# Row buffers by a falling look-ahead, one load for two quads' bases, and a moved base row in a gather-and-scatter graph layer

## The chip, the cores and the metric

The kernel runs on one core of a Trainium2 chip. The metric is the time of one execution on the device in microseconds (us). Three runs of the kernel before gave 1079.93, 1080.61 and 1087.88 us; the median, 1080.61 us, is the time before. Names in the text: PE is the matrix engine (PEld its weight loads), DVE the vector engine, ACT the scalar engine, POOL the GpSimd engine, which here issues the indirect DMAs, and SP the engine that issues most other DMAs.

## The reference

The layer has N = 12500 nodes with 128 features and 400000 edges, sorted by destination. Only edges of length up to 10 count.

```python
rbf = exp(-(d[:, None] - centers) ** 2 / (2 * width * width))       # 50 centres
cut = 0.5 * (cos(pi * d / 10) + 1) * (d <= 10)
W = (silu(rbf @ fw1 + fb1) @ fw2 + fb2) * cut[:, None]
messages = (h[src] @ pw + pb) * W
agg = segment_sum(messages, dst, num_segments=N)
out = layernorm(x + (h + silu(agg @ mw1 + mb1) @ mw2 + mb2))        # h is x
```

## The kernel before, in words

**Packing.** Most edges are too long and are dropped. The edges are cut into seven chunks. `pack_first` (chunk 0) and `pack(c)` shift the edges that stay to the front of each row on DVE, and `columns` writes them as lists to DRAM with one indirect DMA per chunk, the scatter at L470 on POOL's queue. `unpack(c)` (L778) reads the lists back and turns them into what the main loop needs: the source numbers `srci`, the places `dl` of the destinations counted from a base, the factors `cut`, and the row of bases `base_i`. `to_places` (L866) turns an array on PE in one of four PSUM banks and copies it out on DVE (L874); before this change the base row has a turn of its own in another bank (L909 to L913, copy at L912).

**Quads.** The main loop (from L1439) takes 139 quads of 512 edges in order. For quad q it needs the 512 source rows, which POOL gathers with four indirect DMAs of 128 rows (`fetch`, L1009, the DMA at L1015; in eight of the quads the first 128 rows come one by one through SP at L1005 instead), and the filter W from PE and ACT (lines L1056 to L1082). `message(q)` (L1086) multiplies the two on DVE (L1093). `place(q)` (L1100) writes the matrix of destinations, `sum_up(q)` (L1117) multiplies messages by it on PE (L1125), and `add(q)` (L1144) adds the sums into `aggT` at the columns that start at the base, on DVE (L1148). The base is a number in a register: `base_of` (L1130) loads it from `base_i` on DVE's queue (L1134), one load for each window, and a quad has one window up to quad 68 and two from quad 69.

**Row buffers.** `place_of(q)` says which of 21 row buffers quad q is gathered into. Thirteen are `quad_sb`, eight are the tiles `x4_sb` that hold node rows before and after. Up to quad 62 the buffers go round, `q % 21`; from quad 63 nine of them go round. `before_it(q)` is the quad that had the buffer before: the gather of q cannot start until the message of that quad has read it. `room(q)` is how far the gathers may be written into the program ahead of the messages. POOL's queue is in order: gathers in the order of the quads, with the seven scatters between them.

**The order.** The order of the instructions of each engine is fixed when the program is written, by a planner that keeps estimated times: `clock` for DVE, `pool` for POOL, `awake[c]` for the moment from which chunk c's generator may go on. `pack_until` lets the chunks' generators run in the gaps; each `yield` hands back an estimated time. At the end of `pack(c)` chunk 0 is made ready at once (`awake[0] = 0.0`, L774).

**Chunk 0's arrays.** `paired` (L813) keeps chunk 0's placement arrays in the row buffers of quads 11 and 12 (L818): `part`, `f_src` and `f_dl` in that of quad 11, `length`, `two` and `inside` in that of quad 12.

After quad 70 the node layers (lines L1156 to L1212) run between the quads, and a short tail of them follows the last quad.

Of the kernel before, what the change touches and what calls it, by code (L numbers as in the profile page):

```python
# [20 lines left out]
P = 128  # L21
# [29 lines left out]
GOT = 13  # L51
# [18 lines left out]
A_ROW = .58  # L70
AT_ONCE = 32
FROM_BANK = 3


DONE = (0.162, 4.9)
# [5 lines left out]
def kernel(  # L81
# [37 lines left out]
    nc = tc.nc  # L119
    N, H = x.shape  # L120
# [67 lines left out]
    ident = keep.tile([P, P], F32, name="ident")  # L188
    make_identity(nc, ident)
    quad_sb = [keep.tile([P, QT, H], F32, name=f"quad{k}") for k in range(GOT)]  # L190
# [87 lines left out]
    turns, end = (keep.tile([P, 1], F32, name=k) for k in ("turns", "end"))  # L278
# [54 lines left out]
    dl = keep.tile([P, NP, 2], F32, name="dl")  # L333
    base_i = keep.tile([1, NP], I32, name="base_i")
# [24 lines left out]
    def bank(own=None):  # L359

        while not free:
            go_on(next(c for c in held if c != own))
        return free.pop(0)
# [29 lines left out]
    clock = [4.3]  # L393
# [3 lines left out]
    awake = [0.0] * NC_  # L397
# [2 lines left out]
    most = [FROM_X]  # L400
    times = [0]

    def place_of(q):
        n, later = LATER
        return q % len(quad_sb) if q < n else later[(q - n) % len(later)]

    def before_it(q):

# [2 lines left out]
    def room(q):  # L411

        n = q
        while n < NL and before_it(n) < q:
            n += 1
        return n
# [17 lines left out]
    def columns(c, nodes, r_d, first, D, CAP, at_i):  # L434
# [6 lines left out]

        late_c = c >= FROM_BANK
        if late_c:
# [43 lines left out]
    def reach(c, b, bits):  # L487
        return min(ROWS[c] - (1 << b), CAPS[c] + sum(1 << j for j in range(b + 1, bits)))
# [171 lines left out]
    def pack(c):  # L660
# [4 lines left out]
        def rowed(dt, name, n=R, bufs=1):  # L665
            return work.tile([P, max(n, R_MAX) if n == R else max(CAPS)], dt, name=name,
                             bufs=bufs)[:, :n]
# [3 lines left out]
        nc.vector.tensor_copy(first, r_dst[:, 0:1])  # L671
        late_c = c >= FROM_BANK
        if late_c:
# [14 lines left out]
        step = aside.bitcast(I32)[:, :R] if late_c else rowed(I32, "step")  # L688
# [45 lines left out]
        for b in range(bits):  # L734
# [11 lines left out]
            n, k = reach(c, b, bits), 1 << b  # L746
# [24 lines left out]

        yield from columns(c, nodes, r_d, first, 0, CAP, at_i)
        awake[c] = pool[0] + (2.2 if c == 1 else 3.0)
        awake[0] = 0.0  # L774
        yield 0
        yield from unpack(c)

    def unpack(c):  # L778
# [4 lines left out]
        p0, p1 = 2 * QB[c] + (DIRECT // 2 if c == 0 else 0), 2 * QB[c + 1]  # L783
        np_ = p1 - p0
# [28 lines left out]
        def paired(dt, name):  # L813
            if c == 0:
                k = OWN_0[name]
                if k > 3:
                    return dl_0[:np_, k % 2 * 2:k % 2 * 2 + 2].rearrange("p a f -> p (a f)").bitcast(dt)
                v = quad_sb[GOT - 1 - k // 2].rearrange("p j f -> p (j f)").bitcast(dt)  # L818
                return v[:np_, k % 2 * 256:k % 2 * 256 + 256]
            return work.tile([64, 256], dt, name=name, bufs=1)[:np_]  # L820

# [17 lines left out]
        def turned():  # L839
            t = bank()  # L840
            held.append(c)
            return t, t.rearrange("p (j e) -> p j e", j=2)

        def back(t):
            held.remove(c)
            free.append(t)

        def later(more=0.0):

            if c or known[0] >= DIRECT // QT:  # L850
                awake[c] = clock[0] + (5.0 if known[0] >= QB[c + 1] else 1.0 if c == 0 else 2.5) + more
                return 0.0
            return 0.5
# [3 lines left out]
        def lengths():  # L857

            if c < 2:
                alike_in(1)  # L860
            one_of(length, 1)
            for a, b in parts(np_):
                nc.sync.dma_start(near_d[p0 + a:p0 + b], length[a:b].bitcast(F32))
            stored.add(c)

        def to_places(f, to):  # L866
            t, tp = turned()
            for j in range(2):
                nc.tensor.transpose(tp[:, j, :np_], f[:, j * P:(j + 1) * P], ident[:np_, :np_])
            if to is srci:  # L870
                lengths()
                yield 1.4 if c < 2 else 0.8
            yield later(-2.0 if c == 1 and to is srci else 0.0)
            nc.vector.tensor_copy(to[:, p0:p0 + np_, :].rearrange("p r j -> p j r"),  # L874
                                  tp[:, :, :np_])
            back(t)

        yield from to_places(f_src, srci)
# [7 lines left out]
        if mine:  # L886
            at_row = work.tile([64, P], I32, name="at_row", bufs=2)
            nc.vector.tensor_scalar(at_row[:np_], f_src[:, :P], float(4 * H), None, op0=OP.mult)
            for q in mine:
                p = 2 * (q - QB[c])  # L890
# [3 lines left out]
        base = work.tile([64, 1], F32, name="base", bufs=4)[:np_]  # L894
# [3 lines left out]
        if c < WIDE_C:  # L898
            t, tp = turned()
            nc.tensor.matmul(tp[:np_, 0, 0:1], even[:np_, :np_], base, start=True, stop=True)  # L900
            yield later()
            base = work.tile([64, 1], F32, name="base", bufs=4)[:np_]
# [3 lines left out]
        f_dl = paired(F32, "f_dl")  # L906
        nc.vector.tensor_scalar(f_dl, part, base, None, op0=OP.subtract)
        yield from to_places(f_dl, dl)
        t, tp = turned()  # L909
        nc.tensor.matmul(tp[0:1, 0, :np_], base, ident[:np_, :np_], start=True, stop=True)  # L910
        yield later()
        nc.vector.tensor_copy(base_i[:, p0:p0 + np_], tp[0:1, 0, :np_])  # L912
        back(t)  # L913
        yield 2.2
        mark = paired(F32, "mark")
        nc.vector.tensor_scalar(mark, two, float(1 << 2 * SB), -1.0, op0=OP.is_ge, op1=OP.mult)
        if c:
# [62 lines left out]
    def own(q, name, also):  # L980

        k = q % (4 if q >= OWN_4 else 2)
        if k > 1:
            return quad_sb[OTHERS[2 * also + k - 2]]
        if (name, k) not in own_sb:
            own_sb[name, k] = keep.tile([P, QT, H], F32, name=f"{name}{k}")
        return own_sb[name, k]
# [56 lines left out]
    def chunk_of(q):  # L1044
        return max(c for c in range(NC_) if QB[c] <= q)
# [63 lines left out]
    def wide(q):  # L1109

        return WIDE_0 if q < DIRECT // QT else WIDTHS[chunk_of(q)]

    def windows(q):

        return 1 if chunk_of(q) < WIDE_C else 2
# [10 lines left out]
                             start=(j % n == 0), stop=(j % n == n - 1))  # L1126

    bases = {}

    def base_of(q, ks=(0, 1)):  # L1130
        for k in ks:
            if k == windows(q):
                break
            _, v = nc.values_load_multi_w_load_instructions(  # L1134
                base_i[0:1, 2 * q + k:2 * q + k + 1], engines=[mybir.EngineType.DVE],
                min_val=0, max_val=N - wide(q),
                skip_runtime_bounds_check_because="bases are destinations, and end in the table")
            bases[q, k] = v[0]
# [197 lines left out]
    def go_on(c):  # L1336
        v = next(chunks[c], None)
        if v is None:
            todo.remove(c)
        else:  # L1340
            clock[0] += v
# [97 lines left out]
    for q in range(NL - 1):  # L1439
        while todo and q + 2 >= DIRECT // QT and todo[0] <= chunk_of(min(q + 2, NQ - 1)):  # L1440
            go_on(todo[0])
        msg = message(q)
        nodes(q)
        most[0] = room(q)
        fetches(clock[0], most[0])
        fetches(math.inf, min(NL, q + AHEAD + 1))
        assert fetched[0] > QT * min(NL - 1, q + AHEAD)
        if q >= CLEAR_Q:
            clear()
        if loads_later and q >= 8:  # L1450
            nc.sync.dma_start(*loads_later.pop(0))
        radials(q // 2 + 5)
        one_by_one()
        multiplies(q + 1 + EARLY_X)
        if q + 2 < NL:
            second(q + 2)
        if q % 4 < 2 and 2 * octs(q) < NL:
            first(octs(q))
            silu(octs(q))
        if q % 4 == 3:  # L1460
            for o in (q // 4 * 2 + 4, q // 4 * 2 + 5):
                if 2 * o < NL:
                    basis(o)
        if q > NL - 5:
            keep_busy(2)
        sum_up(q, msg)
        now = range(added(q), added(q + 1))
        for k in now:
            base_of(k, (0,))
        if q < NL - 2:  # L1470
            place(q + 1)
        if q == NL - 4:
            place(NL - 1)
        if q == NL - 2:
            for j in range(QT - 1):
                sum_up(NL - 1, message(NL - 1, (j, j + 1)), (j,))
        for k in now:
            base_of(k, (1,))
            if q == NL - 5 and k == now[0]:
                deep.append(deviations([80], st_of[0]))  # L1480
                nc.scalar.activation(warm, half_pi, AF.Silu)
            add(k)
        tail(q)
        clock[0] = max(clock[0], there_at[q])
        summed[q] = clock[0] + 0.7
        clock[0] += 2.2 + 0.3 * (windows(q) - 1)
        if q == 0:
            clear_packed(2, nc.sync)
        if todo:
            pack_until(max(there_at[q + 1], clock[0] + (PACK_US if known[0] >= QB[3] else EARLY_US)), NC_)  # L1490
        if NODES - 8 <= q < NODES - 2:
            part_of(*(("mb1", mb1_f) if q < NODES - 5 else ("mb2", mb2_f)), (q - NODES + 8) % 3)
        if not todo and not counted:
            counted.append(q)
            count()
        elif counted and some is None and fetched[0] >= QT * NL:
            some = nc.values_load(bad_i[0:1, 2:3], min_val=0, max_val=3 * E)
    q = NL - 1
# [131 lines left out]
```

## Time and profile before

| what | value |
|---|---|
| median of three runs | 1080.61 us |
| the profiled execution, its own time | 1084.51 us |
| its span, from the first to the last instruction | 1082.7 us |
| mean granted clock of PE | 0.774 |
| indirect DMAs on POOL | 548 gathers, 7 scatters |

How to read the views: a row of a timeline has the start, the length, the engine, the line, the operation, what it writes and reads, and in brackets how long the engine was idle before it and what ended that. "DVE msg L1093" in brackets means that the wait ended with the message multiplication of that line. A row of the table by stages has a stretch of time and for each engine the time it was busy in it, with the number of instructions.

### The profile page before, as it was taken

Reading aid. Unit: us, or ns where it says so; the run is one execution under the profiler, and the core shown is the slowest. Engines: PE = TensorE matmul, PEld = TensorE weight load, DVE = VectorE, ACT = ScalarE, POOL = GpSimd, SP = SyncE. Lnnn points to the kernel's source line nnn. Section 1 sums busy time; section 2 is a strip of 40 time slices with the busy share of each in tenths; the row PEclk is TensorE's granted clock in tenths of the full one; section 3 lists DMA queues with packets and bytes.
Section 4 is the critical chain, followed back from the end, with each engine's and each line's share of the span. In section 5 each row is a group of like instructions: output and inputs, shape, how many; then the busy total and the mean of one; then the engine's idle time right before and its main releaser. Section 6 shows DMA issues by size and latency. Waiting matters only on the chain. (4 is left out here: it accounts for less than half of the span.)

```text
span 1082.7 us, 13636 instructions
## 1 busy us (share of the span) xinstructions
PE 676.0 (62%) x3531; PEld 527.4 (49%) x3531; DVE 564.8 (52%) x1734; ACT 401.6 (37%) x571; POOL 530.3 (49%) x569
## 2 busy tenths in 40 slices
PE   3665437517464817455788466777766768476785
PEld 3664226406353616334666345555554556354564
DVE  8346509514454816346689465454443534253376
ACT  3334313205222324213445332353352354235365
POOL 6335732456464453754332654655555666563500
PEclk8778557858686957758889877797887878778798
DMA  7563321132222211221212223323222223223312
GB/s 221 183 220 117 112 69 38 40 83 77 57 67 57 79 50 55 71 68 48 84 55 66 76 77 78 85 63 107 78 86 89 81 77 90 72 75 99 86 59 82
DMA packets 53104, 91.38 MB, mean 84 GB/s; under 512 B 13824, under 2 KB 20576, under 8 KB 53018
## 3 DMA queue, kind: packets, MB, share of 16 engines
q1 hardware_dynamic: 34610, 53.34, 15.4%
q0 software_dynamic: 17840, 36.77, 13.2%
q8 instruction: 30, 0.49, 0.2%
q14 instruction: 56, 0.46, 0.1%
q10 hardware_dynamic: 568, 0.33, 0.1%
HBM read 74.59 MB, written 15.79 MB: 83 GB/s over the span
## 5 line engine op out<-in xcount | busy, mean ns | idle before, releaser
L1015 POOL DMA_INDIRECT quad<-proj,srci x405 | 383.7, 947 | 329.9 <-issue 109.4
L1082 PEld LDWEIGHTS bank<-fw_sb,s 128*128 128x128 f32 x1112 | 180.5, 229 | 152.5 <-issue 144.7
L1105 DVE TENSOR_SCALAR hot<-iota_n,dl,cut 128x80 f32<-128x80 f32 (+4 forms) x408 | 110.8, 333 | 203.6 <-remote 107.4
L1071 ACT ACTIVATE s<-ph 128x1024 f32<-128x1024 f32 x70 | 71.2, 1017 | 391.9 <-remote 204.2
L1065 PE MATMUL ph<-rbf,w_sb 102*128 102x512 f32 x278 | 169.5, 738 | 62.3 <-ACT s L1071 45.0
L1082 PE MATMUL bank<-fw_sb,s 128*128 128x128 f32 x1112 | 182.6, 313 | 33.9 <-issue 33.7
L1125 PEld LDWEIGHTS sums<-hot,msg 128*128 128x128 f32 x816 | 120.6, 215 | 79.7 <-issue 56.5
L1125 PE MATMUL sums<-hot,msg 128*128 128x80 f32 (+4 forms) x816 | 121.6, 294 | 37.0 <-issue 24.5
L1079 PE MATMUL bank<-fb_b,ones_b 96*128 96x512 bf16 x139 | 61.7, 444 | 103.7 <-DVE r_d L485 31.8
L1065 PEld LDWEIGHTS ph<-rbf,w_sb 102*128 102x128 f32 x278 | 59.3, 236 | 115.2 <-issue 65.0
L1015 POOL DMA_INDIRECT x<-proj,srci x95 | 90.3, 951 | 49.6 <-issue 26.5
L1148 DVE TENSOR_TENSOR aggT<-aggT,sums 128x80 f32 (+4 forms) x209 | 53.7, 257 | 111.3 <-remote 49.8
L327 PEld LDWEIGHTS bank<-pw_sb,xT 128*128 128x128 f32 (+1 forms) x292 | 50.2, 245 | 64.3 <-issue 41.9
L1093 DVE TENSOR_TENSOR msg<-bank,quad 128x512 f32<-128x512 f32 (+1 forms) x78 | 52.7, 676 | 41.7 <-issue 26.9
L1056 ACT ACTIVATE rbf<-d,rbf_bias,rbf_scale 102x512 f32<-102x512 f32 x70 | 56.2, 802 | 23.4 <-DMA d<-near_d 13.9
L1015 POOL DMA_INDIRECT quad<-in_x_dram,srci x48 | 46.3, 964 | 35.2 <-issue 13.7
L327 PE MATMUL bank<-pw_sb,xT 128*128 128x128 f32 (+1 forms) x292 | 50.9, 331 | 7.5 <-ACT xT L951 7.5
L1093 DVE TENSOR_TENSOR quad<-bank,quad 128x512 f32<-128x512 f32 (+2 forms) x40 | 25.1, 631 | 48.3 <-remote 24.5
L324 PE MATMUL bank<-pb_b,ones_b 96*128 96x512 bf16 (+2 forms) x38 | 17.6, 463 | 51.8 <-issue 22.4
L1125 PE MATMUL sums<-quad,quad 128*128 128x128 f32 (+3 forms) x296 | 46.3, 304 | 5.8 <-issue 5.4
L327 PEld LDWEIGHTS bank<-mw_sb,zs 128*128 128x128 f32 x196 | 32.3, 236 | 34.9 <-issue 18.9
L1125 PEld LDWEIGHTS sums<-quad,quad 128*128 128x128 f32 x296 | 43.9, 224 | 6.9 <-issue 5.9
(268 smaller groups left out, 881.3 us busy)
## 6 DMA issues: line engine op xcount, KB each, us to landing
d<-near_d SPq DMA_DIRECT2D x70, 256.0 KB
dl<-proj SPq DMA_DIRECT2D x1024, 0.5 KB
x<-in_x_dram SPq DMA_DIRECT2D x46, 256.0 KB
quad<-proj,srci POOLq DMA_INDIRECT x405
proj<-hp SPq DMA_DIRECT2D x24, 256.0 KB
out_dram<-x SPq DMA_DIRECT2D x22, 256.0 KB
x<-proj,srci POOLq DMA_INDIRECT x95
r_d<-in_edge_weight_dram SPq DMA_DIRECT2D x5, 256.0 KB
```

Source lines behind the costliest of these rows:

```text
L324: nc.tensor.matmul(to[:m, a:a + c, :], ones_b[:, :m], bias_b[:, :c, :], start=True, stop=False)
L327: nc.tensor.matmul(to[:m, k, :], lT[:, k * P:k * P + m], w, start=False, stop=(k == a + c - 1))
L1015: nc.gpsimd.indirect_dma_start(out=got[:, j, :], out_offset=None, in_=proj if table is None else table, in_offset=bass.IndirectOffsetOnAxi ...
L1056: nc.scalar.activation(rbf[:u], d[:u], AF.Square, bias=rbf_bias[:u], scale=rbf_scale[:u])
L1065: nc.tensor.matmul(ph[:, h, :], w1_sb[:2 * KR, h, :], rbf[:2 * KR], start=True, stop=True)
L1071: nc.scalar.activation(s[:, :n], ph[:, :n], AF.Silu)
L1079: nc.tensor.matmul(pu, ones_b[:, :P], bias_b["fb2"].rearrange("k j f -> k (j f)"), start=True, stop=False)
L1082: nc.tensor.matmul(pu[:, j * H:(j + 1) * H], s[:, j * P:(j + 1) * P], fw2_sb, start=False, stop=(j == QT - 1))
L1093: nc.vector.tensor_mul(msg[:, a:b, :], pu_of[q].rearrange("p (j f) -> p j f", j=QT)[:, a:b, :], got_of[q][:, a:b, :])
L1105: nc.vector.tensor_scalar(hot[:, j, :wide(q)], iota_n[:, :wide(q)], dl[:, at[0], at[1]], cut[:, at[0], at[1]], op0=OP.is_equal, op1=OP.mult)
L1125: nc.tensor.matmul(pa[:, k * W:k * W + wide(q)], msg[:, j, :], hot[:, j, :wide(q)], start=(j % n == 0), stop=(j % n == n - 1))
L1148: nc.vector.tensor_add(to, to, pa[:, k * W:k * W + wide(q)])
```

## The change

It does five things. (1) `place_of` chooses a buffer by a look-ahead `cap`: 20 quads up to quad 33, then one less for every four quads, down to 4 from quad 94; among the allowed buffers whose last quad lies at least `cap` back it takes the one used most recently, and if there is none the one used longest ago. (2) `paired` keeps chunk 0's `part`, `f_src` and `f_dl` in the message tile of odd quads, not in quad 11's row buffer. (3) At the end of `pack(c)` chunk 0 is made ready four planner-us later. (4) `to_places` for `dl` also turns the base row, in the same bank, and copies it right behind; the turn of its own goes. (5) `bases_of` loads the bases of two quads in one load where both have the same width and number of windows, before `place`; else `base_of` stays.

```diff
+LATE_0 = 4.0
...
+    placed = []
+
     def place_of(q):
         n, later = LATER
-        return q % len(quad_sb) if q < n else later[(q - n) % len(later)]
+        while len(placed) <= q:
+            k = len(placed)
+            last = {}
+            for m, b in enumerate(placed):
+                last[b] = m
+            allowed = range(len(quad_sb)) if k < n else later
+            cap = max(4, min(20, 20 - (k - 30) // 4))
+            ok = [b for b in allowed if last.get(b, -99) <= k - cap]
+            never = [b for b in allowed if b not in last]
+            if k < len(quad_sb):
+                placed.append(k)
+            elif ok:
+                placed.append(max(ok, key=lambda b: last.get(b, -99)))
+            else:
+                placed.append(min(allowed, key=lambda b: last.get(b, -99)))
+        return placed[q]
...
-        awake[0] = 0.0
+        awake[0] = clock[0] + LATE_0
...
-                v = quad_sb[GOT - 1 - k // 2].rearrange("p j f -> p (j f)").bitcast(dt)
+                v = quad_sb[GOT - 1] if k < 2 else own(1, "msg", 0)
+                v = v.rearrange("p j f -> p (j f)").bitcast(dt)
...
+            if to is dl:
+                nc.tensor.matmul(tp[0:1, 0, P:P + np_], base, ident[:np_, :np_], start=True, stop=True)
             yield later(-2.0 if c == 1 and to is srci else 0.0)
             nc.vector.tensor_copy(to[:, p0:p0 + np_, :].rearrange("p r j -> p j r"),
                                   tp[:, :, :np_])
+            if to is dl:
+                nc.vector.tensor_copy(base_i[:, p0:p0 + np_], tp[0:1, 0, P:P + np_])
             back(t)
...
         yield from to_places(f_dl, dl)
-        t, tp = turned()
-        nc.tensor.matmul(tp[0:1, 0, :np_], base, ident[:np_, :np_], start=True, stop=True)
-        yield later()
-        nc.vector.tensor_copy(base_i[:, p0:p0 + np_], tp[0:1, 0, :np_])
-        back(t)
-        yield 2.2
+        yield 2.4
...
+    def bases_of(quads_now):
+
+        a, n = quads_now[0], 2 * len(quads_now)
+        step = 2 // windows(a)
+        _, v = nc.values_load_multi_w_load_instructions(
+            base_i[0:1, 2 * a:2 * a + n].rearrange("o (w t) -> o w t", t=step)[:, :, 0],
+            engines=[mybir.EngineType.DVE], min_val=0, max_val=N - wide(quads_now[-1]),
+            skip_runtime_bounds_check_because="bases are destinations, and end in the table")
+        for i, (q, k) in enumerate((q, k) for q in quads_now for k in range(windows(q))):
+            bases[q, k] = v[i]
...
         now = range(added(q), added(q + 1))
-        for k in now:
-            base_of(k, (0,))
+        at_once = len(now) == 2 and wide(now[0]) == wide(now[1]) and windows(now[0]) == windows(now[1])
+        if at_once:
+            bases_of(list(now))
+        else:
+            for k in now:
+                base_of(k, (0,))
...
         for k in now:
-            base_of(k, (1,))
+            if not at_once:
+                base_of(k, (1,))
```

## The prediction

> **What bounds the kernel now.** I read the page first, then POOL's waits, then the stages in which POOL gathers without a pause.
>
> ```profile
> span 1082.7 us, 13636 instructions
> PE 676.0 (62%) x3531; PEld 527.4 (49%) x3531; DVE 564.8 (52%) x1734; ACT 401.6 (37%) x571; POOL 530.3 (49%) x569
> ```
>
> No engine is busy for more than 62% of the span, so the time lies in waits. Gathers are not late and take the same time throughout:
>
> ```profile
> DVE msg L1093 <- DMA quad<-proj,srci: 6.7, 3, 2.7
> POOL quad L1015 <- DVE msg L1093: 104.5, 21, 20.3
> ...
> L1015 POOL DMA_INDIRECT quad<-proj,srci x405: 938/944/1187, 105.0 to 1027.9; - x135
> ```
>
> Messages waited for gathers 6.7 us in all, while POOL waited for messages, that is for a free row buffer, 104.5 us. POOL is ahead and stands at the limit of its buffers. What hurts is what a run of gathers does to the others. Back to back, gathers start every 1.25 us (0.94 and a gap of 0.30). Ten runs of twelve gathers between 588 and 976 us, first the first 8 us of each (two rows and the sum), then the stretch from 9 to 16.5 us behind its start:
>
> ```profile
> core 0: us, PE busy (x) PEld busy (x) DVE busy (x) ACT busy (x) POOL busy (x), PEclk, DMA share, GB/s
> 607.90:615.90 8.00, 8.00 (x46) 7.54 (x46) 7.71 (x26) 6.41 (x9) 6.17 (x7) 0.68 0.44 114
> 959.50:967.50 8.00, 5.70 (x38) 4.47 (x37) 7.14 (x27) 0.21 (x1) 6.15 (x7) 1.00 0.27 79
> sum 80.00, PE 72.02 PEld 57.19 DVE 67.15 ACT 34.77 POOL 61.70; mean PE 7.20 PEld 5.72 DVE 6.71 ACT 3.48 POOL 6.17
> ```
>
> ```profile
> 616.90:624.40 7.50, 1.51 (x10) 1.05 (x8) 0.00 (x0) 0.00 (x0) 4.42 (x5) 0.92 0.20 54
> 968.50:976.00 7.50, 4.84 (x14) 2.74 (x15) 0.00 (x0) 2.57 (x3) 4.46 (x5) 0.58 0.19 53
> sum 75.00, PE 24.62 PEld 16.30 DVE 8.23 ACT 15.53 POOL 44.65; mean PE 2.46 PEld 1.63 DVE 0.82 ACT 1.55 POOL 4.47
> ```
>
> DVE is busy 84% of the heads (67.15 of 80) and 11% of the tails (8.23 of 75); PE falls from 90% to 33%. So a run of gathers is harmless for some 9 us and then brings the other engines nearly to a stand until it has ended. The cause is not in these rows; the rule is. Long runs cost most. Three of them, from the ninth us on, and the messages within the whole run:
>
> ```profile
> 315.30:329.20 13.90, 2.19 (x13) 2.38 (x13) 0.31 (x1) 0.00 (x0) 9.20 (x10) 0.65 0.26 68
> 376.50:399.40 22.90, 3.13 (x17) 2.90 (x17) 0.00 (x0) 0.01 (x1) 15.90 (x17) 0.60 0.28 85
> 443.50:470.00 26.50, 6.39 (x14) 3.48 (x14) 0.78 (x2) 0.02 (x1) 18.70 (x20) 0.54 0.20 52
> ```
>
> ```profile
> core 0: us, DVE busy (x), PEclk, DMA share, GB/s
> 306.30:329.20 22.90, 2.02 (x3) 0.79 0.26 74
> 367.50:399.40 31.90, 2.03 (x3) 0.71 0.30 92
> 434.50:470.00 35.50, 2.04 (x3) 0.66 0.24 67
> ```
>
> Three messages each, all in the head. A run is therefore as long as the buffers that are free when it starts, and the three that the head frees.
>
> **The change, part by part.**
>
> *Row buffers.* POOL's position is counted from the messages and gathers done:
>
> ```profile
> 0.00:434.50 434.50, 24.89 (x37) 0.73 0.32 95
> 0.00:510.40 510.40, 31.57 (x47) 0.72 0.31 91
> 0.00:588.10 588.10, 42.93 (x64) 0.74 0.30 87
> ...
> 0.00:434.50 434.50, 206.04 (x216) 0.73 0.32 95
> 588.10:1030.90 442.80, 249.95 (x264) 0.80 0.29 83
> ```
>
> (The first three rows are messages, the last two gathers.) At 434.5 us 37 messages are done, quads 0 to 36, and 216 gathers, which is into quad 54. The run that starts there has 27 indirect DMAs: three quads that found free buffers, three that the head freed, and what was left of quad 54. POOL had been held up before it:
>
> ```profile
> 367.53 0.94 POOL L1015 DMA_INDIRECT quad<-proj,srci  x1 [9.05 <-DVE at_row L888]
> 434.50 0.99 POOL L470 DMA_INDIRECT packed<-line,at_i  x1 [17.07 <-DVE first L671]
> 528.06 0.94 POOL L1015 DMA_INDIRECT quad<-proj,srci  x1 [17.67 <-DVE msg L1093]
> 588.18 0.94 POOL L1015 DMA_INDIRECT quad<-proj,srci  x1 [20.26 <-DVE msg L1093]
> ```
>
> By the new rule a quad's buffer was last used 20 quads back up to quad 33, 18 at quads 38 to 41, 16 at 46 to 49, 15 at 50 to 53, 14 at 54 to 57, 12 at 62; quads 63 to 71 find buffers idle for 9 or more, then it is 9 to quad 77, 5 at 90, 4 from 94. So at 434.5 us POOL could have got no further than quad 51, whose buffer quad 36 has just left. No buffer is free in store, and the run is the three quads of its head, twelve gathers. I take the same for the runs at 367.5 and 306.3 us, where the rule gives 17 and 18.
>
> *What a run costs.* A tail of 7.5 us loses 6.5 us by DVE (0.82 busy against 84% of 7.5) and 4.8 by PE (2.46 against 90%): 5.7 for a run of twelve. A run of eight ends after 9.7 us; I estimate 1.0 for it. The three long tails are 63.3 us, lost to 98% by DVE and 79% by PE: 56 us for some 66 gathers. As runs of twelve the same gathers cost 5.5 x 5.7 = 31, as runs of eight 8.2 x 1.0 = 8. **Gain: 25 to 48 us.**
>
> *What is given back.* The number of gathers stays. Before, the store falls from 21 quads to 9 at one place, the waits of 17.67 and 20.26 us above. There the work ran undisturbed: 17 messages between 510.4 and 588.1 us (64 less 47), 4.6 us each. After, nine of those twelve steps have been used up earlier, so 36 more gathers fall there: three runs of twelve, 17 us, or 4.5 of eight, 4.5 us. At the end the last gather goes out at 1027.9 us now, and the last eight quads run without gathers:
>
> ```profile
> 1031.00:1068.00 37.00, 32.86 (x205) 25.92 (x205) 28.63 (x107) 28.26 (x49) 0.00 (x0) 0.95 0.20 69
> ```
>
> They take 4.6 us each. With four quads in store 20 gathers move into this stretch: 9.5 us or 2.5. Those 20 leave the stretch between quads 78 and 93: minus 9.5 or 2.5. The sum is a gain of 25 - 17 - 9.5 + 9.5 = 8 us if the runs are of twelve and 48 - 4.5 - 2.5 + 2.5 = 43.5 if they are of eight. For eights speaks that from quad 34 to 93 the store shrinks by 16 in 60 quads, so in most cycles of three messages one frees nothing for a gather; against it, that from quad 94 nothing shrinks and cycles stay as now. I take the middle, **26 us**.
>
> The added wait stands in POOL's queue; behind it are later gathers and the scatters of chunks 3 to 6. The scatter of chunk 4 went out at 434.5 us, and its first quad, 69, is the 70th message, behind the 64 done at 588.1: over 150 us of cover.
>
> A rule of the Trainium skill (SBUF — State Buffer, "The 'DVE blocks DMA' trap (SWDGE)") has the harm run the other way: DVE in a two-port mode locks GpSimd out, and descriptors come late. The row of gathers disagrees: minimum 938, median 944 ns, with DVE idle or not. By the page gathers would stretch beside DVE work, and a small store would expose that; it would take the gain away.
>
> *The front.* Chunk 0 wakes four us later, its arrays leave quad 11's buffer, the base row joins the turn of `dl`.
>
> ```profile
> 92.85 0.18 DVE L874 COPY dl<-bank 128x20 f32<-128x20 f32 x1 [5.96 <-PE bank L869]
> ...
> 102.54 0.94 POOL L1015 DMA_INDIRECT quad<-in_x_dram,srci  x1 [6.87 <-PE bank L696]
> 111.55 0.94 POOL L1015 DMA_INDIRECT x<-proj,srci  x1 [1.57 <-DVE srci L874]
> 118.54 0.69 DVE L1093 TENSOR_TENSOR msg<-bank,quad 128x512 f32<-128x512 f32 x1 [2.43 <-issue]
> L912 DVE CAST base_i<-bank 1x44 int32<-1x44 f32 (+4 forms) x7 | 1.2, 176 | 1.1 <-PE bank L910 1.1
> ```
>
> DVE stood 5.96 us before the copy of chunk 0's `dl`; with the later waking, chunk 2's packing fills that. It gains at most 6 us, and if the loop's start hangs on PE and ACT alone, nothing. It loses at most the same if the bank of `dl`, held that much longer, is missing to the projections (four banks). Two gathers of quad 11 no longer wait until 102.54; quad 12 still waits for `length` and `inside`. No message waits for these rows, as the 6.7 us above say; what counts is that gathers end sooner before the run at 111. **2 us of gain, from -6 to +6.** The base row's own turn cost one wait of 1.1 us in seven chunks, in gaps: nothing, from 0 to 2.
>
> *Base loads.*
>
> ```profile
> L1134 DVEq TENSOR_LOAD <-base_i x209: 296/306/573, 174.4 to 1067.4; - x105
> L1001 SPq TENSOR_LOAD <-at_row x32: 673/2126/2377, 113.3 to 1004.4; - x32
> DVE aggT L1148 <- issue: 7.9, 17, 1.6
> ```
>
> Before, 209 loads at 306 ns, 64 us of DVE's queue. SP's loads of 32 numbers take 2126 ns, so each further number costs some 59 ns. After, 61 pairs take one load (34 of two numbers at 0.37, 27 of four at 0.48) and 33 windows stay single: 36 us. The 28 us lie beside running DVE work; at most the 7.9 us that adds stood on "issue" are theirs. **1 us, from 0 to 8.** The chain's last load, of quad 138, stays single.
>
> **Sum.** 26 + 2 + 1 = 29 us. The profiled execution took 1084.5 us by its own time, 3.9 over the median and within the three runs shown: 1084.5 - 29 = 1055.5, so **1055 us**, its own range 1042 to 1068.
>
> **The rivals.**
>
> *All eights* (1030 us). Every run shrinks to eight or fewer: 43.5, with the front and loads at 11. For it: the shrinking store. Against: where the store is constant, ten runs of twelve stand among the 264 gathers from 588 us on, at a store of nine.
>
> *Runs form again* (1079 us). The runs are twelves everywhere, because three messages fit into a head: 8 + 3 = 11 less a front that loses 6. For it: the last argument. A look-ahead that isn't binding would come out here too; against that, POOL's 104.5 us of waits for messages.
>
> *The quiet stretch is lost* (1105 us, slower). The long runs stay, since they start from POOL's waits for a chunk's list or scatter (9.05 and 17.07 us), during which messages free buffers whatever the limit. Then 17 + 9.5 are paid, 2.5 come back, 3 for the rest: 1084.5 + 21 = 1105. It decides at 434 us: whether POOL there stands for the scatter with buffers free, or for a message. Against: the count above gives no free buffer.
>
> **How the numbers follow.** Chances: 0.5 for the forecast, 0.13 all eights, 0.2 runs form again, 0.17 quiet stretch lost. The range 1026 to 1088 takes in all but the last. About 1% (1070 to 1091) is what a measurement here tells from no change. Faster by more: the forecast almost whole and the eights, 0.61; within: 0.22; slower: 0.17.
>
> **What would show it.** Right: no run over 16 gathers after 300 us; the tails at 376 to 399 and 443 to 470 us gone with messages in their place; waits of 17 and 20 us for messages replaced by many short ones; the last gather within 25 us of the last message; some 94 base loads. Wrong: runs of 20 and more between 350 and 480 us; messages that wait for gathers (over 30 us in all); DVE and PE busy in tails; the loop's first message later than 118.54 us, its row above, by more than 6.

## The result, and the profile after

The changed kernel took 1052.51 us (median of 6 runs, 1036.08 to 1058.75), the kernel before beside it 1084.91 us (6 runs, 1079.93 to 1087.88): a ratio of 0.963, with a 95% interval of 0.957 to 0.969. The forecast was 1055 us. The profiled execution took 1050.97 us, 33.5 us less than the one before. Its page:

```profile
span 1049.2 us, 13515 instructions
PE 672.1 (64%) x3531; PEld 520.4 (50%) x3531; DVE 564.9 (54%) x1734; ACT 403.2 (38%) x572; POOL 530.4 (51%) x569
```

Every engine does the work that it did before, so all that went is waiting. POOL's waits show how it is held now:

```profile
POOL quad L1033 <- DVE msg L1111: 112.2, 23, 14.2
POOL quad L1033 <- DVE quad L1111: 75.3, 16, 14.7
POOL packed L488 <- DVE first L689: 39.3, 3, 31.8
```

L1033 is the gather and L1111 the message in the new line numbers (L1015 and L1093 before); in some quads the message is written into the row buffer itself, which is the second row. The third row is a chunk's scatter that waits for its list. POOL waits for messages more often, and its longest such wait is 14.7 us, where the rows of before had 17.67 and 20.26. The place of the long run of 434.5 us, and one of the two longest runs behind 300 us:

```profile
407.03 0.99 POOL L488 DMA_INDIRECT packed<-line,at_i  x1 [4.98 <-DVE first L689]
428.75 1.01 POOL L1033 DMA_INDIRECT quad<-proj,srci  x1 [5.72 <-DVE hot L1123]
...
534.34 0.97 POOL L1033 DMA_INDIRECT quad<-proj,srci  x1 [5.77 <-DVE msg L1111]
```

The scatter of chunk 4 goes out at 407.03 us and twelve gathers follow it, the three quads of the head; before it was 26 gathers. The longest runs behind 300 us are now of 16, at 534.34 and 813.7 us; before they were of 24 and 27. Most of what is left of a run past its ninth microsecond looks as it did. Three tails, from the ninth us to the last gather (of the runs at 534.34, 587.39 and 912.2 us), then the sum over the tails of all fourteen runs of twelve and more behind 300 us, and last the same sum over the fifteen such runs of the kernel before:

```profile
543.30:554.00 10.70, 5.53 (x21) 3.88 (x20) 2.33 (x6) 1.02 (x1) 8.26 (x9) 0.84 0.21 55
...
596.40:602.20 5.80, 5.33 (x22) 3.23 (x21) 5.30 (x13) 0.73 (x1) 4.57 (x5) 0.74 0.52 148
...
921.20:926.90 5.70, 0.00 (x0) 0.00 (x0) 0.00 (x0) 2.02 (x3) 4.48 (x5) 0.50 0.38 104
sum 99.30, PE 36.70 PEld 26.71 DVE 18.78 ACT 14.55 POOL 77.59; mean PE 2.62 PEld 1.91 DVE 1.34 ACT 1.04 POOL 5.54
```

```profile
sum 125.40, PE 35.53 PEld 25.80 DVE 11.32 ACT 16.64 POOL 97.25; mean PE 2.37 PEld 1.72 DVE 0.75 ACT 1.11 POOL 6.48
```

DVE is busy 19% of the tails (18.78 of 99.30) and PE 37%; before it was 9% (11.32 of 125.40) and 28%. The tails are nearly as many and shorter in all. Most are as hard as before, but not each: in the tail of the run at 587.39 us DVE is busy for 5.30 of 5.80 us, so a run of twelve need not end in a stand. Between 300 and 500 us, where the long runs were, DVE is now busy for 125.03 us and before for 98.41.

The time by quads shows where it came from. Each row is the stretch between the starts of two messages (quads 0, 16, 40, 64, 78, 94, 130 and 138), with the gathers that POOL issued in it in brackets; first before, then after:

```profile
core 0: us, POOL busy (x), PEclk, DMA share, GB/s
118.52:298.23 179.71, 85.01 (x90) 0.70 0.24 67
298.23:475.34 177.11, 89.87 (x95) 0.71 0.21 62
475.34:591.46 116.12, 42.45 (x45) 0.83 0.23 67
591.46:683.09 91.63, 50.76 (x55) 0.80 0.29 78
683.09:797.47 114.38, 62.17 (x66) 0.81 0.29 81
797.47:1031.25 233.78, 134.35 (x142) 0.80 0.30 86
1031.25:1068.03 36.78, 0.00 (x0) 0.95 0.19 67
```

```profile
121.63:284.85 163.22, 74.80 (x80) 0.70 0.24 67
284.85:414.80 129.95, 70.43 (x75) 0.78 0.26 74
414.80:564.86 150.06, 70.99 (x75) 0.76 0.23 64
564.86:654.16 89.30, 47.57 (x51) 0.84 0.27 76
654.16:748.60 94.44, 46.62 (x50) 0.82 0.30 86
748.60:987.10 238.50, 135.15 (x143) 0.80 0.30 89
987.10:1033.89 46.79, 18.89 (x20) 0.85 0.24 71
```

In these two profiles the same work of the other engines takes longer or shorter as more or fewer gathers fall beside it. Quads 16 to 40 lost 20 gathers and 47 us; quads 40 to 64 got 30 gathers and 34 us; the last eight quads got 20 gathers and 10 us. A gather moved away from quads 0 to 40 is worth 1.6 to 2.4 us (16.49 / 10, 47.16 / 20), one between quads 78 and 94 1.2 us (19.9 / 16); one moved into quads 40 to 64 costs 1.1 us (33.9 / 30), one moved to the end 0.5 us (10.0 / 20). These are shares of a stretch's difference, not measurements of one gather. The change gains by the difference of these prices: fewer gathers stand where they came in runs of 20 and more.

### The profile page after: what moved, and what is told of

The parts are those of the page before. It is cut to its first block, busy times and chain, and to the rows that moved or that the text cites. A ratio compares the mean times of both kernels' runs of the same rounds, so it can differ in the third digit from the quotient of the medians.

```text
span 1049.2 us, 13515 instructions
## 1 busy us (share of the span) xinstructions
PE 672.1 (64%) x3531; PEld 520.4 (50%) x3531; DVE 564.9 (54%) x1734; ACT 403.2 (38%) x572; POOL 530.4 (51%) x569
## 5 line engine op out<-in xcount | busy, mean ns | idle before, releaser
L1033 POOL DMA_INDIRECT quad<-proj,srci x421 | 398.9, 948 | 341.5 <-DVE msg L1111 112.2
L1100 PEld LDWEIGHTS bank<-fw_sb,s 128*128 128x128 f32 x1112 | 176.3, 225 | 125.8 <-issue 114.3
L1083 PE MATMUL ph<-rbf,w_sb 102*128 102x512 f32 x278 | 176.8, 769 | 85.0 <-ACT s L1089 57.0
L1100 PE MATMUL bank<-fw_sb,s 128*128 128x128 f32 x1112 | 177.4, 309 | 16.2 <-issue 16.2
L1143 PEld LDWEIGHTS sums<-hot,msg 128*128 128x128 f32 x816 | 125.3, 222 | 64.2 <-issue 48.8
L1143 PE MATMUL sums<-hot,msg 128*128 128x80 f32 (+4 forms) x816 | 124.3, 300 | 19.5 <-issue 12.1
L1033 POOL DMA_INDIRECT x<-proj,srci x79 | 75.0, 950 | 62.5 <-DVE msg L1111 28.9
L1111 DVE TENSOR_TENSOR msg<-bank,quad 128x512 f32<-128x512 f32 (+1 forms) x82 | 55.4, 676 | 41.5 <-remote 21.0
L1033 POOL DMA_INDIRECT quad<-in_x_dram,srci x48 | 46.8, 976 | 29.4 <-issue 13.7
L1111 DVE TENSOR_TENSOR quad<-bank,quad 128x512 f32<-128x512 f32 (+2 forms) x40 | 25.1, 632 | 48.6 <-remote 44.9
L1143 PE MATMUL sums<-quad,quad 128*128 128x128 f32 (+3 forms) x296 | 42.3, 283 | 9.8 <-issue 7.9
L969 ACT COPY xT<-bank 128x512 f32<-128x512 f32 (+1 forms) x37 | 21.2, 578 | 64.5 <-remote 44.5
```

Of the source, the lines that this page charges most:

```text
L969: nc.scalar.copy(xT[:, :n], xp[:, :n])
L1033: nc.gpsimd.indirect_dma_start(out=got[:, j, :], out_offset=None, in_=proj if table is None else table, in_offset=bass.IndirectOffsetOnAxi ...
L1083: nc.tensor.matmul(ph[:, h, :], w1_sb[:2 * KR, h, :], rbf[:2 * KR], start=True, stop=True)
L1100: nc.tensor.matmul(pu[:, j * H:(j + 1) * H], s[:, j * P:(j + 1) * P], fw2_sb, start=False, stop=(j == QT - 1))
L1111: nc.vector.tensor_mul(msg[:, a:b, :], pu_of[q].rearrange("p (j f) -> p j f", j=QT)[:, a:b, :], got_of[q][:, a:b, :])
L1143: nc.tensor.matmul(pa[:, k * W:k * W + wide(q)], msg[:, j, :], hot[:, j, :wide(q)], start=(j % n == 0), stop=(j % n == n - 1))
```

## The experiments

**The theory** is that of the prediction: a run of gathers without a pause brings the other engines to a stand after some 9 us, so the price depends on the length of the runs. **The rivals**: the front or the base loads carry the gain; what counts is the number of gathers in a stretch, or their mean pace, and not that they stand back to back. The experiments met chips of two kinds, and this was the main surprise: on two chips the kernel before took 1094 and 1097 us, near the 1085 of the result; on three others it took 728 to 730 us. Ratios are always to the kernel before on the same chip.

**The buffers alone.** The kernel before with the new `place_of`.

```diff
-        return q % len(quad_sb) if q < n else later[(q - n) % len(later)]
...
+            cap = max(4, min(20, 20 - (k - 30) // 4))
...
+        return placed[q]
```

> The kernel before with the new choice of row buffers alone (front, base row and base loads as before). Theory (the buffers carry nearly all): 26 to 32 us under before, so 1050 to 1060 us; the 40th quad's message within 15 us of the 414.8 us that it has in the changed kernel; no run of more than 16 gathers after 300 us. Rival (front, base row and base loads carry 10 us or more): 1064 to 1075 us.

1077.24 us against 1096.82: ratio 0.981 (0.972 to 0.989). The gain of 20 us is under the expected 26 to 32, quad 40's message starts at 434.7 us and not within 15 of 414.8, and the longest run is of 17. The rival's 1064 to 1075 us isn't reached either, but the kernel before is 12 us slower here than beside the result (1096.82 for 1084.91). Read as gains, 20 us lies in the rival's 10 to 21 and under the theory's 26 to 32, but the interval (12 to 31 us) doesn't tell the two apart. What the other parts carry is decided by the next run.

**Everything but the buffers.** The changed kernel with the old `place_of`.

```diff
+        return q % len(quad_sb) if q < n else later[(q - n) % len(later)]
...
-        return placed[q]
```

> The changed kernel with the old choice of row buffers (so front, base row and base loads alone). Theory: 1079 to 1086 us, that is 0 to 6 us under before, with the long runs of gathers near 306, 367 and 434 us still there and messages standing in them. Rival: these parts carry 10 us or more, 1064 to 1075 us, which would also show as an earlier start of the long runs.

1096.72 us: ratio 0.999 (0.995 to 1.004). Two of the three long runs are back (24 gathers each, from 373.94 and 444.17 us; at 304.67 us stands one of 13), and so are the stands; their tails from the ninth us on:

```profile
382.90:403.80 20.90, 3.93 (x19) 3.61 (x20) 1.44 (x3) 0.00 (x0) 15.97 (x17) 0.57 0.30 89
...
453.20:474.00 20.80, 2.14 (x9) 1.96 (x9) 3.48 (x8) 4.25 (x6) 15.88 (x17) 0.60 0.23 63
```

The front, the base row and the base loads together are worth nothing that can be measured. The rival that they carry the gain is out.

This run and the buffers alone ran on the same chip, one with the old and one with the new buffers (their fronts and base loads differ too), so the prices can be taken once more. Quads 0 to 16 fell from 178.40 us (90 gathers) to 166.59 (82), quads 16 to 40 from 178.17 (95) to 149.17 (77); quads 40 to 64 rose from 120.52 (45) to 145.60 (72), the last eight from 35.24 (0) to 47.25 (20). That is 1.5, 1.6, 0.9 and 0.6 us a gather, in the same order as above. Quads 78 to 94 don't repeat: 109.60 us (66) and 108.06 (57), 0.2 us a gather where the result's profiles gave 1.2.

**The whole change on such a chip.** The changed kernel again, on another of the chips that show the stands.

> The changed kernel once more beside the kernel before. On a chip on which the kernel before takes about 1090 us and runs of gathers bring the other engines to a stand: if the buffers alone (0.981, 0.972 to 0.989) are the whole change, a ratio of 0.975 to 0.987; if the parts help one another, 0.957 to 0.969. On a chip on which it takes about 728 us: 0.995 to 1.005 again.

1066.81 us against 1094.17: ratio 0.974 (0.963 to 0.986). It overlaps with the result's 0.957 to 0.969 and with the buffers alone (0.972 to 0.989), so it can't decide between them. Those two don't overlap: the buffers alone gained 1.9% on their chip and the whole change 3.7% on that of the result, though the other parts alone are worth nothing. Whether the parts help one another or the chips differ stays open. By the stretches (quads 16 to 40: 141.56 us with 77 gathers; 40 to 64: 146.34 with 72; the last eight: 46.66 with 20) it repeats the profile above.

**A floor of nine.**

```diff
-            cap = max(4, min(20, 20 - (k - 30) // 4))
+            cap = max(9, min(20, 20 - (k - 30) // 4))
```

> The changed kernel with a look-ahead that falls to nine quads in place of four (nothing differs before quad 75). Theory of the prediction (a fixed store of any size gives runs of twelve; what a falling store gains between quads 78 and 93 is given back in the last eight quads): 1047 to 1056 us, the same as the changed kernel within 1%, with 30 us less gained between quads 68 and 94 or about 10, and about 10 us less given back in the last eight quads. Rival (a small store itself shortens the runs, so that the 30 us between quads 68 and 94 are kept to the end): 1065 to 1080 us.

1084.42 us against 1096.82: ratio 0.985 (0.978 to 0.992), no different from the 0.981 of the buffers alone on the same chip; the absolute 1047 to 1056 us was missed with the chip's own level. Quads 64 to 78, 78 to 94 and the last eight, with the gathers in brackets; then the same stretches of the buffers alone, which ran with a floor of four on the same chip:

```profile
588.73:683.53 94.80, 52.81 (x57) 0.75 0.26 74
683.53:793.32 109.79, 59.97 (x64) 0.80 0.29 83
...
1031.79:1068.71 36.92, 0.00 (x0) 0.95 0.17 59
```

```profile
580.31:668.03 87.72, 42.04 (x45) 0.84 0.28 76
668.03:776.09 108.06, 53.82 (x57) 0.78 0.27 78
...
1014.43:1061.68 47.25, 18.99 (x20) 0.86 0.24 71
```

With a floor of nine the last eight quads have no gathers and take 36.92 us; with four they have 20 and take 47.25 here, 46.79 in the result's profile. So the 10 us given back at the end belong to these gathers. In return four buys 9 us between quads 64 and 94 on this chip (195.78 for 204.59 us), which is the theory's "about 10". The seven stretches together take 942.78 us with nine and 942.73 with four, and the 7 us between the two medians lie ahead of the first message in the profiles (125.93 and 118.95 us), where the floor plays no part. Set against the result's profile (183.74 us from quad 64 to 94) and the repeat's (187.17), four would have bought 21 and 17 us. The rival wanted some 12 to 28 us over the change. The change itself didn't run on this chip; by its ratios of 0.963 and 0.974 elsewhere I estimate 1056 or 1068 us for it here, 28 or 16 less than the floor of nine. So the same chip speaks for the theory, and the rival isn't out.

**A store of three, early.**

```diff
-            cap = max(4, min(20, 20 - (k - 30) // 4))
+            cap = max(3, min(20, 20 - 2 * (k - 21)))
```

> The changed kernel with a look-ahead that falls by two quads per quad from quad 21 and stays at three quads from quad 30. On a chip that shows the stands: theory (the length of a run sets the price, and a store of three lets a run go on for twelve gathers at most behind the last message) 1010 to 1045 us, with no run of over sixteen gathers behind 200 us; rival (a store so small makes messages wait for gathers where POOL stands for a chunk's scatter) 1060 to 1110 us. On a chip without them, where POOL's gathers follow each other without a pause for 720 us: 726 to 740 us by the theory, since the store is empty there anyway; 745 to 780 us if the waits for a message now stand in the way of the gathers.

1067.68 us (1048.04 to 1074.38, too scattered for an interval) beside 1066.81 for the change and 1094.17 before: the theory's 1010 to 1045 is missed. The time lies in the rival's 1060 to 1110, but without the rival's reason: messages waited 0.5 us for gathers. The theory's sign failed too: one run of 23 gathers starts at 513.56 us, quads 60 to 65, of which the last three find buffers idle for 39 quads and more. The store is used up earlier, and the total stays, as far as four scattered times can tell: what quads 0 to 16 save (128.91 us with 43 gathers) quads 40 to 64 give back (177.10 us with 95).

**Pauses on POOL.** This tests the theory without touching a buffer: the kernel before, with four writes of one row of 512 numbers after every second quad.

```diff
+            if j == QT - 1 and q % 2 and q >= 13:
+                for _ in range(4):
+                    nc.gpsimd.iota(rest_i, pattern=[[1, 512]], base=0, channel_multiplier=0)
```

> The kernel before, buffers and all else as they are, with four short writes of one row on POOL (about 2.2 us in all) after the last gather of every second quad from quad 13, so that no run has more than eight gathers back to back. Theory (the unbroken length of a run is what brings the other engines to a stand): the stands near 376 to 399 and 443 to 470 us go, messages come between, and the time is 1035 to 1065 us although POOL has some 140 us more to do. Rival (what counts is how many buffers are free, or the number of gathers in a stretch, not that they are back to back): no gain or a loss, 1080 to 1110 us, with the stands still there.

951.70 us against 1096.82: ratio 0.865 (0.857 to 0.873), where the change has 0.963 and 0.974, and this although POOL has 138 us more to do. The direction was expected, the size not: the theory's 1035 to 1065 us counted the long runs alone, and the pauses break the runs of twelve and those ahead of 300 us as well.

```profile
PE 665.3 (70%) x3531; PEld 517.6 (55%) x3531; DVE 568.3 (60%) x1734; ACT 402.5 (42%) x571; POOL 671.1 (71%) x821
...
L430 POOL IOTA rest_i<- 1x512 int32 x252 | 138.0, 547 | 13.4
```

The pace, from POOL's trace, is eight gathers and a pause of 2.4 us (the last gather of a run, the pause and the next run's first):

```profile
354.96 0.94 POOL L1019 DMA_INDIRECT quad<-proj,srci  x1 [0.30 <-issue]
355.90 2.38 POOL L430 IOTA rest_i<- 1x512 int32 x4
358.46 0.98 POOL L1019 DMA_INDIRECT quad<-proj,srci  x1 [0.17 <-issue]
```

And quads 0 to 16 and 16 to 40, with the gathers:

```profile
122.68:249.54 126.86, 77.17 (x81) 0.80 0.30 86
249.54:375.49 125.95, 75.41 (x79) 0.81 0.27 76
```

Quads 0 to 16 have 81 gathers beside them, as many as in the changed kernel (80), and take 126.86 us in place of 163.22. So the number of gathers doesn't set the price. Nor does their pace: with pauses POOL issues 502 gathers in the 798.7 us from 108.5 on (0.63 per us), without them 495 in the 916.4 us from 111.5 on (0.54 per us). The gathers come faster and harm less, because behind 122 us no run has more than nine. Nor is it how many buffers are free: POOL waited 10.2 us for messages, where it was 104.5 in the row of before, so with pauses it nearly always found one. The long stands are gone: between 300 and 500 us DVE is busy for 143.13 us, in the profile of the kernel before for 98.41. Both rivals are out on a chip of this kind.

**The other kind of chip.** The changed kernel, the same pauses on it, one tiny write in place of each pause, and pauses of double length behind every fourth quad went to a chip where the kernel before takes 728.46 us.

> The changed kernel once more, on the chip of the other runs of this set, so that the parts can be put beside the whole. If the buffers alone (ratio 0.981, 0.972 to 0.989, with the other parts measured at nothing) are the change, the ratio is 0.975 to 0.987; if the parts help one another, it stays at 0.957 to 0.969.

729.10 us: ratio 1.001 (0.999 to 1.004). The change does nothing here. Its page, and the stretch from 31.4 us to 464.1 us, one unbroken run of 343 indirect DMAs:

```profile
span 727.0 us, 13515 instructions
PE 586.3 (81%) x3531; PEld 460.7 (63%) x3531; DVE 560.9 (77%) x1734; ACT 402.4 (55%) x572; POOL 533.0 (73%) x569
```

```profile
31.40:464.10 432.70, 350.79 (x2118) 280.47 (x2119) 373.59 (x1087) 227.49 (x304) 328.35 (x343) 0.91 0.41 120
```

DVE is busy for 86% of it and PE for 81%, beside gathers at the same pace (328.35 / 343 = 0.96 us each). There is no stand. POOL's gathers are themselves the bound, which messages wait for, so the store is empty whatever its limit:

```profile
DVE msg L1111 <- DMA quad<-proj,srci: 42.4, 17, 4.3
DVE quad L1111 <- DMA quad<-proj,srci: 20.5, 14, 2.8
```

The same pauses in the changed kernel, on this chip:

> The changed kernel with the same pauses on POOL behind every second quad. Theory (breaking the runs is all that the small store did): the pauses do its work, and a store of four only makes POOL wait where it was paced already, so no faster than the pauses on the kernel before, 950 to 985 us. Rival (the two add up, since the store also stops POOL where messages are behind): 915 to 940 us.

874.78 us: ratio 1.2005 (1.197 to 1.204). Pauses on POOL where POOL is the bound cost all that they take. Whether pauses and small store add up where there are stands, this run cannot say.

One tiny write, beside the pauses above:

```diff
-                for _ in range(4):
-                    nc.gpsimd.iota(rest_i, pattern=[[1, 512]], base=0, channel_multiplier=0)
+                for _ in range(1):
+                    nc.gpsimd.iota(rest_i[:, :1], pattern=[[1, 1]], base=0, channel_multiplier=0)
```

> The kernel before with one write of a single number on POOL (about 0.15 us) after every second quad from quad 13, in place of the pause of 2.2 us. Theory (it is the pause that lets the other engines go on, so the time without gathers counts): little, 1060 to 1100 us. Rival (any instruction of another kind between gathers breaks whatever builds up): 950 to 1000 us.

728.89 us: ratio 1.001 (0.999 to 1.003). Nothing is left to break here, so time or instruction stays undecided by this run.

Pauses of double length:

```diff
-            if j == QT - 1 and q % 2 and q >= 13:
-                for _ in range(4):
+            if j == QT - 1 and q % 4 == 3 and q >= 13:
+                for _ in range(8):
```

> The kernel before with the same writes on POOL, but eight of them (about 4.5 us) after every fourth quad, so that the mean pace is that of the kernel with pauses and the runs have sixteen gathers. Theory (length of a run): each run has a tail of some 10 us again, and the time is 1010 to 1080 us. Rival (the mean pace of the gathers): 945 to 970 us.

873.75 us: ratio 1.199 (1.196 to 1.201), the cost of the pauses again. The same kernel ran twice more, on two more chips of this kind (873.20 us against 728.91, 873.75 us against 730.25):

> The kernel before with eight writes on POOL (about 4.5 us) after every fourth quad once more, for a chip on which the kernel before takes about 1090 us and runs of gathers bring the other engines to a stand. There: theory (length of a run) 1010 to 1080 us, with a tail of some 10 us in runs of sixteen gathers; rival (the mean pace of the gathers) 945 to 970 us. On a chip on which the kernel before takes about 728 us: 868 to 880 us as in the run before, which tells nothing of the two.

> The kernel before with eight writes on POOL (about 4.5 us) after every fourth quad, a third time. On a chip on which the kernel before takes about 1090 us: theory (length of a run) 1010 to 1080 us, with a tail of some 10 us in runs of sixteen gathers; rival (the mean pace of the gathers) 945 to 970 us. On a chip on which it takes about 728 us: 868 to 880 us again, which tells nothing of the two.

So longer runs at the same mean pace weren't tried where they would hurt. There the pace is ruled out by the rates above.

## Why the prediction was right, point by point

The sum was 29 us and the profiles differ by 33.5; the mechanism held on the chips that show the stands. The signs that the prediction named came true in the profile: no run of over 16 gathers behind 300 us, messages in place of the long tails, a longest wait of 14.7 us for a message, and the last gather 14 us ahead of the last message. "The repeat" in the terms is the changed kernel on another chip, set against the same profile of the kernel before.

- **The long runs of 306, 367 and 434 us: taken 25 to 48, measured 47 (36 in the repeat).** Quads 16 to 40 fell from 177.11 to 129.95 us (141.56 in the repeat); with the old and the new buffers on one chip it was 29. The count of POOL's position was right: no buffer was free when the scatter went out, and twelve gathers followed it.
- **Before 300 us: taken as nothing, measured 16.5.** This step failed. Quads 0 to 16 went from 179.71 to 163.22 us and lost 10 gathers. The rule gives quads 21 to 33 a look-ahead of 20 in place of 21; the run at 211.1 us had 20 gathers, and now one of 16 starts at 213.5.
- **Given back in the quiet stretch: taken 17 or 4.5, measured 34 (30 in the repeat).** The prediction moved 36 gathers there, and 30 came (72 - 45 = 27 in the repeat). The size of one was wrong: at 5.7 us for a run of twelve a gather is 0.5 us, and it cost 1.1.
- **Quads 78 to 93: taken 9.5 or 2.5, measured 20.** 16 gathers left, at 1.2 us each and not at 0.5. That a tail costs more than its own idle time, since the chain of the engines must start again behind it, would explain both, but it is only argued; and on the chip of the buffers alone this term was under 2 us.
- **The end: taken 9.5 for twenty gathers, measured 10.0 for twenty.** The floor of nine, without gathers there, shows that it is theirs.
- **The front: taken as a gain of 2, measured as a loss of 3 to the first message.**

```profile
94.66 0.18 DVE L895 COPY dl<-bank 128x20 f32<-128x20 f32 x1 [2.85 <-PE bank L967]
...
114.37 0.94 POOL L1033 DMA_INDIRECT x<-proj,srci  x1 [7.37 <-DVE srci L895]
121.65 0.69 DVE L1111 TENSOR_TENSOR msg<-bank,quad 128x512 f32<-128x512 f32 x1 [2.34 <-PE bank L1100]
```

DVE's wait ahead of the `dl` copy shrank from 5.96 to 2.85 us as meant. But POOL then stood 7.37 us for chunk 1's sources, which came at 114.37 and not at 111.55, and the first message followed, 121.65 for 118.54. That was within the range of -6 to +6, but the chip of the experiments repeats neither. With the new front DVE waited 11.62 and 13.18 us for the `dl` copy (everything but the buffers, floor of nine), with the old one 7.46 (the buffers alone), and the first message came at 125.31 and 125.93 us, not at 118.95. So the prediction's sign of being wrong, a first message more than 6 us later than 118.54, was met there. The total of everything but the buffers doesn't show it (0.999, 0.995 to 1.004), and no profile of the kernel before on that chip tells where it was made good.

- **Base loads: taken 1, not seen.**

```profile
L1152 DVEq TENSOR_LOAD <-base_i x61: 340/508/973, 178.8 to 1015.9; - x61
L1163 DVEq TENSOR_LOAD <-base_i x33: 297/305/558, 610.8 to 1033.3; - x33
...
DVE aggT L1177 <- issue: 0.5, 2, 0.3
```

94 loads, as counted, a pair at a median of 508 ns (estimated 370 and 480). The 7.9 us that adds stood on "issue" went to 0.5 in the result's profile, but with the same loads and the old buffers they were 6.8, and with the old loads and the new buffers 6.2. So it isn't shown that the loads removed them.

The rule cited from the Trainium skill (SBUF — State Buffer, "The 'DVE blocks DMA' trap (SWDGE)") isn't borne out: gathers have a median of 944 ns with stands and without, with DVE at 54% and at 77%.

That the forecast came so near is in part luck, because two misses cancelled. The gain ahead of quad 40 was taken at 36.5 us, the middle of 25 and 48, and measured 64 in these profiles; what quads 40 to 64 give back was taken at 11, the middle of 17 and 4.5, and measured 34.

## What to carry to other kernels

Where the bound is many waits and no engine, look at what a stretch has beside it, not only at what it waits for: here a gather cost from 0.2 to 2.4 us by the place that it left or entered, and most where the runs were longest. When work only moves, count it in the stretch that it leaves and in the one that it enters, each at the price of that place. And take a tuned schedule to a second chip before carrying its rule on: on three chips the effect that this change works against wasn't there, and pauses that gained 13% in the kernel before on one chip cost 20% in the changed kernel on another.

## What the runs showed of the hardware

The stand differs between the chips, or between the hours: each set of runs ran on its own chip and at its own time. The kernel before took 1094 and 1097 us on two chips and 728 to 730 on three; the gathers are the same on both kinds (a median of 944 ns). In a stand, instructions that wait for nothing come late. PE in the run of 27 of the kernel before:

```profile
454.39 0.37 PE L1082 MATMUL bank<-fw_sb,s 128*128 128x128 f32 x1 [1.73 <-issue]
456.49 0.37 PE L1082 MATMUL bank<-fw_sb,s 128*128 128x128 f32 x1 [1.73 <-issue]
459.99 0.37 PE L1082 MATMUL bank<-fw_sb,s 128*128 128x128 f32 x1 [3.13 <-issue]
```

Matmuls of 0.37 us start 2.1 to 3.5 us apart, and the profile names no semaphore as their releaser. DVE's next instruction in this run, at 460.71 us, came 18.77 us late, put down to "issue" too. The clearest sign is on SP, whose queue loads single rows at this time and runs one MOVE, a register instruction, beside each. The MOVEs beside the first 9 us of this run, those beside its tail, and those of the changed kernel on a chip without stands (count, then shortest, median and longest in ns):

```profile
L1005 SPq MOVE dl<-proj x15: 3/21/398, 434.6 to 443.1; - x15
...
L1005 SPq MOVE dl<-proj x11: 3/699/1393, 444.5 to 465.6; - x11
...
L1023 SPq MOVE dl<-proj x1024: 29/29/38, 78.5 to 665.2; - x171
```

A register move that takes 29 ns elsewhere has a median of 699 ns in the tail, on an engine that doesn't issue those gathers. So it isn't a chain of waits between engines that stands; instructions themselves go slowly on several engines at once. The transfers aren't what is full: from 443 to 470 us they keep the 16 DMA engines 20% busy, and none of the queues that the page calls "instruction" moves anything. The granted clock of PE differs between the kinds of chip too (0.774 in the kernel before, 0.923 in the changed kernel without stands), but a move on SP is no work of PE. With pauses the longest MOVE is still 967 ns, and that kernel takes 77 us more than the changed kernel with the same pauses on a chip without stands (951.70 for 874.78), so with runs of eight a part of the difference is left.

What is short in a stand, and why one chip has it and another hasn't, stays open. So does whether a pause must be long: a single short write was only tried where there is no stand.
